# Shifted tokens as whole rows in their own tile, a quarter of the sine products on VectorE, and a new order of steps, in a twelve-layer local-attention stage

## The chip, the cores and the metric

The kernel runs on one core of one Trainium2 chip. A core has five engines with an instruction queue each, and every queue is worked off in order: TensorE (PE in the profile, with its weight loads as PEld), VectorE (DVE), ScalarE (ACT), GpSimd (POOL) and SyncE (SP). SP only starts transfers here; POOL starts some too. Sixteen DMA engines carry the transfers. Matrix products go to PSUM, which this kernel uses as eight banks of 512 numbers in each of 128 partitions; everything else lies in SBUF. The metric is the device time of one execution in microseconds (us). The kernel before took 4753.31 us (median of 3 runs, 4749.81 to 4759.05).

## The reference, cut to what matters

The input x is four sequences of 512 tokens of 128 numbers, in float32. The parts in their order: a mixture-of-experts feed-forward and a linear attention (the front), a stack of six local-attention layers, a full attention of sixteen heads, and the six-layer stack once more. The second and the last part are the same code, and they are where the change lies. One layer of it is

```python
def shift_tokens(t):
    a, s = jnp.split(t, 2, -1)
    s = jnp.pad(s, ((0, 0), (1, 0), (0, 0)))[:, :-1]
    return jnp.concatenate([a, s], -1)
...
q = l2norm(q) * qs
k = l2norm(k) * ksc
...
q = q * cos * scale + rotate_half(q) * sin * scale
k = k * cos * inv + rotate_half(k) * sin * inv
out = local_attention(q, k, v)
...
for i in range(DEPTH):
    x = attn_layer(shift_tokens(x), Wqkv[i], q_scale[i], k_scale[i], Wo[i]) + x
    x = ffn_layer(shift_tokens(x), ln_g[i], ln_b[i], W1[i], b1[i], W2[i], b2[i]) + x
```

Two things matter below. Each sublayer reads numbers 0 to 63 of a token and numbers 64 to 127 of the token before it, with zeros for the token before the first. And queries and keys get a rotary embedding: the projection times a cosine table, plus the projection of the partner number times a sine table.

## The kernel before, in words

**Data.** `x[b]` is a tile of 128 partitions by 4 by 128: token 128·t + p of sequence b lies in partition p, row t. So the token before lies one partition higher up, except for partition 0, which needs partition 127 of row t - 1.

**Work.** A layer is worked off for each sequence b in two halves `hf` of eight heads. Each half is a `Unit`, whose methods are generators of steps (a `yield` ends a step):

- `proj(c)`, c = 0 to 7: chunk c of the keys (c = 0 to 3, s = 0) or queries (c = 4 to 7, s = 1). Step 0 makes three matmuls (lines 279 to 281) into a PSUM bank; step 1 copies the bank to the tile `raw` (ACT, line 305); step 2 squares it (ACT, `sq`, line 308); step 3 multiplies the bank by the cosine table (DVE, line 313, into `rtk` or `rtq`); step 4 multiplies `raw` by the sine table (POOL, line 315).
- `swap(s)`: two transfers started by POOL (line 395) add `raw`, with even and odd partitions exchanged, onto `rtk` or `rtq`. It needs all four chunks of s.
- `norm`, `norm_q`: lengths of keys and queries (matmuls of lines 326 and 360 into bank `n2`, a transpose on DVE, logarithm and exponential on ACT, corrections on DVE, lines 342 to 347). `spread` multiplies the keys by their inverse lengths (line 386 on PE, line 389 on DVE).
- `score(k, h)`: masks and scores (lines 425 and 434) into the one bank pair `S`; `soft(k)`: softmax (DVE lines 444 and 446, POOL 449, ACT 451, DVE 454 and 456, POOL 458, DVE transpose 461).
- `vproj(i)`: values, already multiplied by the output weights (PE 407, ACT copy 413); `out(k)`: attention times values (PE 477); `add`: onto `x[b]` (DVE 484).

After both halves of a sequence a `Ffn` follows. Its step `stats` 0 has SP start two transfers that fetch the shifted half of the tokens (lines 606 and 607); step 1 takes means and variances (DVE, lines 612, 614, 615); step 2 the logarithm and exponential (ACT, line 618); step 3 normalizes (POOL, lines 624 to 633); steps 4 to 6 transpose (PE 637, ACT 640, DVE 642). Then come `gate`, `gelu`, `lin` (three steps each, the last one into bank `fout`, line 685) and `fadd` (DVE 692), which frees the bank of `fout`.

**Buffers.** All matmul results but `n2`, `S` and `av` share four PSUM banks `mm` that go round in the order of the program. A step that takes a bank waits until the readers of the fourth result before it are done. `S` has one buffer: the next `score` waits until `soft` step 0 has read the last.

**Order.** For this stage the order is written out by hand. Each step has a due time in the table `TIMES`, by name and half, to which the position of the half in the sequence of halves is added; `Events.at` raises it to the time of every step that it waits for, and all steps are emitted in the order of the resulting times. Since every engine works its queue in order, this sets what stands behind what. Steps of one sequence overlap with those of the next: while the feed-forward of sequence b begins, the second half of sequence b + 1's attention is under way. One period of this order, one sequence in one layer, is two halves; there are 48 periods.

Of the kernel before, what the change touches and what calls it, by code (L numbers as in the profile page):

```python
# [6 lines left out]
F32 = mybir.dt.float32  # L7
# [3 lines left out]
ALU = mybir.AluOpType  # L11
# [109 lines left out]
def setup_l1(g, c):  # L121

    nc, P = g.nc, g.const
# [15 lines left out]

    g.wp = g.ctx.enter_context(g.tc.tile_pool(name="l1w", bufs=1))  # L140
# [4 lines left out]
    def fill():  # L145
# [4 lines left out]
        nc.gpsimd.memset(g.ge2[64:128], 1.0)  # L150
        NEG = -1.0e25
# [132 lines left out]
class Unit:  # L284
# [8 lines left out]
    def proj(self, c):  # L293
        g = self.g
        nc = g.nc
        xT = g.xT[(self.l, self.b)]
        s, i = c // 4, c % 4
        ps = bank(g, "mm", [128, 512], "qkps")
# [5 lines left out]
        raw = self.raw[s][:, i, :]  # L304
        nc.scalar.copy(raw, ps)  # L305
# [6 lines left out]
        rot = g.rot[(self.l, s)]  # L312
        nc.vector.tensor_tensor(self.rt[s][:, i, :], ps, rot[:, 0, :], ALU.mult)  # L313
        yield
        nc.gpsimd.tensor_tensor(raw, raw, rot[:, 1, :], ALU.mult)  # L315
# [171 lines left out]
    def events(self, ev, u):  # L487
# [3 lines left out]
        def go(fn, *args, **wait):  # L491
            ev.steps(u, (fn.__name__, hf) + args, (key, fn.__name__) + args, fn(*args),
                     {int(n[1:]): [x if isinstance(x[0], tuple) else (key,) + x for x in xs] for n, xs in wait.items()})

        P = ev.before
        for c in range(8):
            go(self.proj, c, s0=[((l, b), "xT", 2), ((l, hf), "qk", c, 2)],
               s1=[("proj", c // 4 * 4, 1)] if c % 4 else [],
               s3=[((l,), "rot", c // 4, 1)] + ([("proj", c // 4 * 4, 3)] if c % 4 else []))
# [3 lines left out]
        for s in range(2):  # L503
            go(self.swap, s, s0=[("proj", c, t) for c in range(4 * s, 4 * s + 4) for t in (3, 4)])
# [17 lines left out]
class Events:  # L522
# [30 lines left out]
    ('proj', 0, 0): (0.505, 0.505, 0.505, 0.505, 0.505), ('proj', 1, 0): (0.375, 0.375, 0.375, 0.406, 0.406),  # L553
    ('proj', 0, 1): (0.789, 0.789, 0.789, 0.789, 0.789), ('proj', 1, 1): (0.582, 0.582, 0.582, 0.582, 0.582),
    ('proj', 0, 2): (0.722, 0.722, 0.722, 0.722, 0.722), ('proj', 1, 2): (0.466, 0.466, 0.466, 0.466, 0.466),
    ('proj', 0, 3): (0.728, 0.728, 0.728, 0.728, 0.728), ('proj', 1, 3): (0.339, 0.375, 0.375, 0.406, 0.406),
    ('proj', 0, 4): (0.925, 0.925, 0.925, 0.925, 1.025), ('proj', 1, 4): (0.795, 0.795, 0.795, 0.795, 0.795),
    ('proj', 0, 5): (1.063, 1.063, 1.063, 1.063, 1.353), ('proj', 1, 5): (0.901, 0.901, 0.901, 0.901, 0.901),
    ('proj', 0, 6): (0.961, 0.961, 0.961, 0.961, 0.961), ('proj', 1, 6): (0.668, 0.795, 0.795, 0.795, 0.795),
    ('proj', 0, 7): (1.072, 1.072, 1.072, 1.072, 1.072), ('proj', 1, 7): (0.932, 0.932, 0.932, 0.932, 1.330),  # L560
    ('norm', 0): (1.020, 1.020, 1.112, 1.337, 1.337, 1.443), ('norm', 1): (0.843, 0.843, 0.843, 0.971, 1.057, 1.197),
    ('norm_q', 0): (1.466, 1.492, 1.492, 1.701, 1.701), ('norm_q', 1): (1.079, 1.571, 1.571, 1.754, 1.754),
    ('swap', 0, 0): (0.789,), ('swap', 1, 0): (0.582,), ('swap', 0, 1): (1.353,), ('swap', 1, 1): (1.330,),
    ('spread', 0, 0): (1.443, 1.443), ('spread', 1, 0): (1.582, 1.586), ('spread', 0, 1): (1.443, 1.443),
    ('spread', 1, 1): (1.443, 1.443), ('spread', 0, 2): (1.443, 1.443), ('spread', 1, 2): (1.197, 1.197),
    ('spread', 0, 3): (1.660, 1.660), ('spread', 1, 3): (1.197, 1.197), ('score', 0, 0, 0): (1.838,),
    ('score', 1, 0, 0): (1.881,), ('score', 0, 0, 1): (1.838,), ('score', 1, 0, 1): (1.881,),
    ('soft', 0, 0): (1.838, 2.074, 2.074, 2.074, 2.376, 2.565),
    ('soft', 1, 0): (1.881, 1.881, 2.044, 2.119, 2.119, 2.230), ('score', 0, 1, 0): (2.034,),
    ('score', 1, 1, 0): (2.044,), ('score', 0, 1, 1): (2.034,), ('score', 1, 1, 1): (2.044,),  # L570
    ('soft', 0, 1): (2.034, 2.301, 2.415, 2.415, 2.415, 2.586),
    ('soft', 1, 1): (2.044, 2.044, 2.171, 2.171, 2.243, 2.243), ('vproj', 0, 0): (1.875, 1.875),
    ('vproj', 1, 0): (2.169, 2.169), ('vproj', 0, 1): (2.135, 2.135), ('vproj', 1, 1): (2.169, 2.169),
    ('vproj', 0, 2): (2.135, 2.135), ('vproj', 1, 2): (2.261, 2.261), ('vproj', 0, 3): (2.135, 2.339),
    ('vproj', 1, 3): (2.261, 2.261), ('vproj', 0, 4): (2.135, 2.339), ('vproj', 1, 4): (2.261, 2.261),
    ('vproj', 0, 5): (2.428, 2.428), ('vproj', 1, 5): (2.261, 2.261), ('vproj', 0, 6): (2.428, 2.428),
    ('vproj', 1, 6): (2.261, 2.261), ('vproj', 0, 7): (2.428, 2.428), ('vproj', 1, 7): (2.261, 2.261),
    ('out', 0, 0): (2.839,), ('out', 1, 0): (2.422,), ('out', 0, 1): (2.839,), ('out', 1, 1): (2.422,),
    ('out', 0, 2): (2.839,), ('out', 1, 2): (2.422,), ('out', 0, 3): (3.161,), ('out', 1, 3): (2.422,),
    ('add', 0): (3.161,), ('add', 1): (2.422,), ('stats',): (2.828, 2.828, 2.828, 2.828, 3.037, 3.037, 3.037),  # L580
    ('gate', 0): (3.443, 3.443), ('lin', 0): (3.894, 3.894, 4.830), ('gate', 1): (3.443, 3.443),
    ('lin', 1): (3.894, 3.894, 4.830), ('gate', 2): (3.894, 3.894), ('lin', 2): (4.055, 4.055, 4.830),
    ('gelu',): (3.894,), ('aside',): (1.053,), ('fadd',): (4.830,), ('xT',): (-0.063, -0.063, 0.230),
    ('fw',): (4.307, 4.347, 4.347, 4.347), ('rot', 0): (-5.173, -5.173), ('rot', 1): (0.853, 0.853),
    ('qk', 0, 0): (-0.273, -0.273, -0.273), ('qk', 1, 0): (-0.135, -0.135, -0.135),
    ('qk', 0, 1): (-0.266, -0.266, -0.266), ('qk', 1, 1): (-0.287, -0.287, -0.287), ('qk', 0, 2): (0.033, 0.033, 0.208),
    ('qk', 1, 2): (0.405, 0.405, 0.405), ('qk', 0, 3): (-2.849, -1.272, -1.272), ('qk', 1, 3): (-0.698, -0.698, -0.698),
    ('qk', 0, 4): (0.366, 0.366, 0.366), ('qk', 1, 4): (-0.246, -0.246, -0.246), ('qk', 0, 5): (-1.224, -0.937, -0.937),
    ('qk', 1, 5): (0.637, 0.637, 0.637), ('qk', 0, 6): (-0.738, -0.738, -0.738), ('qk', 1, 6): (0.271, 0.271, 0.271),
    ('qk', 0, 7): (-1.136, -0.928, -0.928), ('qk', 1, 7): (0.767, 0.767, 0.767), ('lvo', 0): (1.549,),  # L590
    ('lvo', 1): (1.889,), ('vo', 0, 0): (1.549, 1.549), ('vo', 1, 0): (1.889, 1.889), ('vo', 0, 1): (1.549, 1.549),
    ('vo', 1, 1): (1.889, 1.889),
# [3 lines left out]
class Ffn:  # L596
# [4 lines left out]
    def stats(self):  # L601
        g = self.g
        nc, xb = g.nc, g.x[self.b]
        xs = tile_of(g, "xs", [128, 4, 64], F32, "xs")
        nc.vector.memset(xs[0:1, 0, :], 0.0)
        nc.sync.dma_start(out=xs[1:128], in_=xb[0:127, :, 64:128])
        nc.sync.dma_start(out=xs[0:1, 1:4, :], in_=xb[127:128, 0:3, 64:128])
# [757 lines left out]
```

## Time and profile before

| | |
|---|---|
| runs | 4749.81, 4753.31, 4759.05 us |
| the profiled execution | 4747.36 us, span 4745.6 us, granted PE clock 0.903 |
| PE busy | 3911.9 us, 82% |
| DVE, ACT, POOL busy | 3077.8, 2666.3, 2687.7 us |
| the two six-layer stages | about 600 to 2390 and 2935 to 4746 us from the start |

The profile is that of one execution; times in it are counted from the start of its span. A group of instructions is a line of the kernel with its engine, the tiles it writes and reads, its count, its busy time and mean duration, and what ended the idle time before it. The chain that ended last is followed back from the end: at each step to the instruction or transfer that released it. The view of waits adds up idle time by who waited for whom. PEclk is the share of PE's full clock that was granted. Where successive instructions of an engine overlap a little, their spacing is smaller than their duration, and sums along a path go by the spacing.

In the stage of interest, 300 us of it (3303 to 3603) hold PE 250.5, DVE 184.9, ACT 172.6 and POOL 199.7 us of work.

### The profile page before, as it was taken

Reading aid. Unit: us, or ns where it says so; the run is one execution under the profiler, and the core shown is the slowest. Engines: PE = TensorE matmul, PEld = TensorE weight load, DVE = VectorE, ACT = ScalarE, POOL = GpSimd, SP = SyncE. Lnnn points to the kernel's source line nnn. Section 1 sums busy time; section 2 is a strip of 40 time slices with the busy share of each in tenths; the row PEclk is TensorE's granted clock in tenths of the full one; section 3 lists DMA queues with packets and bytes.
Section 4 is the critical chain, followed back from the end, with each engine's and each line's share of the span. In section 5 each row is a group of like instructions: output and inputs, shape, how many; then the busy total and the mean of one; then the engine's idle time right before and its main releaser. Section 6 shows DMA issues by size and latency. Waiting matters only on the chain.

```text
span 4745.6 us, 150287 instructions
## 1 busy us (share of the span) xinstructions
PE 3911.9 (82%) x66374; PEld 2632.2 (55%) x66436; DVE 3077.8 (65%) x5759; ACT 2666.3 (56%) x5242; POOL 2687.7 (57%) x2630
## 2 busy tenths in 40 slices
PE   8989878788787888888769998878888788787876
PEld 5666556555565555656523333556556555555654
DVE  6968856566565666656668885656656556665665
ACT  4434455556565555655536676555656555565653
POOL 4625576667666666666500002666676666766664
PEclk9989989898898989989879998989989898898988
DMA  2000043333333333333332222334233342323331
GB/s 57 18 9 19 28 99 69 80 63 72 78 63 81 72 72 72 68 77 73 68 80 63 71 68 54 70 68 87 58 85 68 68 85 60 83 61 72 83 68 42
DMA packets 163854, 312.47 MB, mean 66 GB/s; under 512 B 41304, under 2 KB 125664, under 8 KB 138176
## 3 DMA queue, kind: packets, MB, share of 16 engines
q0 software_dynamic: 31008, 202.40, 21.8%
q1 hardware_dynamic: 132192, 100.44, 7.5%
q8 instruction: 521, 8.54, 0.7%
q14 instruction: 133, 1.09, 0.1%
HBM read 77.49 MB, written 17.69 MB: 20 GB/s over the span
## 4 chain that ended last, share of the span: by engine, by line
PE 41%; DMA 19%; DVE 19%; ACT 7%; POOL 7%; issue 6%; SPq 0%; POOLq 0%; ACTq 0%; DVEq 0%
DMA xs<-x 18%; PE vps L407 11%; PE av L477 5%; PE S L434 3%; DVE h L944 3%; DVE E L446 3%; DVE mx L444 3%; PE av L1193 3%; POOL raw L315 2%; PE S L1156 2%; PE n L360 2%; POOL E L458 2%; PE ST L1185 2%; ACT raw L305 2%; ACT sq L308 1%
## 5 line engine op out<-in xcount | busy, mean ns | idle before, releaser
L315 POOL TENSOR_TENSOR raw<-raw,rot 128x512 f32<-128x512 f32 x768 | 1036.0, 1433 | 300.4 <-ACT raw L305 300.4
L407 PE MATMUL vps<-vo,xF 128*32 128x256 f32 x12288 | 787.4, 408 | 57.1 <-DVE ge L679 43.1
L413 ACT COPY vx<-vps 128x512 f32<-128x512 f32 x768 | 445.4, 588 | 413.6 <-PE vps L407 404.8
L407 PEld LDWEIGHTS vps<-vo,xF 128*32 128x32 f32 x12288 | 427.2, 119 | 351.6 <-issue 86.7
L305 ACT COPY raw<-qkps 128x512 f32<-128x512 f32 x768 | 455.7, 593 | 236.7 <-PE qkps L281 231.0
L458 POOL TENSOR_TENSOR E<-E,smr 128x1024 f32<-128x1024 f32 x192 | 391.0, 2070 | 151.4 <-ACT vx L413 90.3
L308 ACT ACTIVATE sq<-qkps 128x512 f32<-128x512 f32 x768 | 475.9, 620 | 0.0
L389 DVE TENSOR_TENSOR rtk<-rtk,R 128x512 f32<-128x512 f32 x384 | 248.4, 678 | 319.9 <-PE R L386 319.9
L449 POOL TENSOR_TENSOR E<-E,rq 128x1024 f32<-128x1024 f32 x192 | 367.9, 1916 | 134.7 <-DVE E L446 129.4
L313 DVE TENSOR_TENSOR rtk<-qkps,rot 128x512 f32<-128x512 f32 x384 | 258.1, 683 | 212.7 <-ACT sq L308 210.2
L477 PE MATMUL av<-vx,pt 128*32 128x128 f32 x11904 | 367.7, 274 | 18.0 <-DVE pt L461 11.8
L1157 DVE TENSOR_REDUCE nm<-S 128x1 f32<-128x512 f32 x512 | 337.4, 686 | 63.9 <-PE S L1156 59.3
L279 PE MATMUL qkps<-xT,wqk 128*128 128x512 f32 x768 | 337.2, 439 | 43.6 <-DVE rtk L313 22.7
L477 PEld LDWEIGHTS av<-vx,pt 128*32 128x32 f32 x11904 | 326.8, 110 | 75.8 <-issue 39.0
L1186 ACT ACTIVATE E<-ST 128x512 f32<-128x512 f32 x512 | 280.4, 595 | 127.3 <-PE ST L1185 103.3
L434 PE MATMUL S<-rtk,rtq 64*32 64x64 f32 (+1 forms) x24576 | 316.0, 243 | 33.8 <-issue 32.0
L313 DVE TENSOR_TENSOR rtq<-qkps,rot 128x512 f32<-128x512 f32 x384 | 255.0, 682 | 133.4 <-ACT sq L308 133.4
L434 PEld LDWEIGHTS S<-rtk,rtq 64*32 64x32 f32 x24576 | 302.2, 114 | 58.8 <-issue 48.0
L618 ACT ACTIVATE y<-bmv,eps 128x4 f32<-128x4 f32 x48 | 14.3, 297 | 564.7 <-DVE bmv L615 564.7
L946 POOL TENSOR_TENSOR h<-r,h 128x512 fp32r<-128x512 f32 x128 | 182.0, 1422 | 252.5 <-DVE h L944 238.5
L280 PE MATMUL qkps<-xT,wqk 128*128 128x512 f32 x768 | 307.9, 401 | 4.3 <-POOL xT L274 2.4
L614 DVE BATCH_NORM_STATS2 bst<-xs 128x6 f32<-128x64 f32 x192 | 35.8, 186 | 424.6 <-DMA xs<-x 424.6
(259 smaller groups left out, 8755.9 us busy)
## 6 DMA issues: line engine op xcount, KB each, us to landing
rtk<-raw POOLq DMA_DIRECT2D x192, 512.0 KB, 7.0
rtq<-raw POOLq DMA_DIRECT2D x192, 512.0 KB, 6.2
pd<-pc SPq DMA_DIRECT2D x36, 384.0 KB
rot<-in_c_rot SPq DMA_DIRECT2D x24, 512.0 KB
wqkr<-in_L_ffn_Wqk SPq DMA_DIRECT2D x192, 64.0 KB
k<-pd SPq DMA_DIRECT2D x32, 288.0 KB
r<-in_L_ffn_W SPq DMA_DIRECT2D x32, 256.0 KB
wvraw<-in_L_ffn_WvT SPq DMA_DIRECT2D x24, 256.0 KB
```

Source lines behind the costliest of these rows:

```text
L279: nc.tensor.matmul(out, lhsT=wh, rhs=xh, start=True, stop=False)
L305: nc.scalar.copy(raw, ps)
L308: nc.scalar.activation(sq, ps, AF.Square)
L313: nc.vector.tensor_tensor(self.rt[s][:, i, :], ps, rot[:, 0, :], ALU.mult)
L315: nc.gpsimd.tensor_tensor(raw, raw, rot[:, 1, :], ALU.mult)
L407: nc.tensor.matmul(ps[p * 32:(p + 1) * 32, ww, :], lhsT=xF[:, t0:t0 + 32], rhs=g.vo[(self.l, self.hf, p // 2)][:, p % 2, :], start=True, s ...
L413: nc.scalar.copy(self.v[th][:, 2 * t:2 * t + 2, :], ps)
L434: nc.tensor.matmul(self.S[k][p * 32:(p + 1) * 32, ab, w * 64 + 64 - n:w * 64 + 64], lhsT=self.rt[1][rows, p, t0:t0 + 32], rhs=self.rt[0][r ...
L449: nc.gpsimd.tensor_tensor(E4, E4, self.rq[:, :, 8 * k:8 * k + 8].unsqueeze(3).to_broadcast([128, 2, 8, 64]), ALU.mult)
L458: nc.gpsimd.tensor_tensor(E, E, r.unsqueeze(2).to_broadcast([128, 16, 64]), ALU.mult)
L477: g.nc.tensor.matmul(self.av[ww * 32:(ww + 1) * 32, k, :], lhsT=self.pt[w // 8][:, ab, w % 8, role, :], rhs=self.v[src // 8][:, src % 8, a ...
L1157: nc.vector.tensor_reduce(self.nm[:, h, qt:qt + 1], S, AX.X, ALU.max, negate=True)
```

## The change

It does three things. The diff, with the table of due times cut:

```diff
+    g.xs = P.tile([128, 4, 128], F32, name="xs")
...
+        nc.gpsimd.memset(g.xs[0:1, 0, :], 0.0)
...
     def proj(self, c):
...
-        nc.scalar.copy(raw, ps)
+        if i == 3:
+            nc.vector.tensor_tensor(raw, ps, g.rot[(self.l, s)][:, 1, :], ALU.mult)
+        else:
+            nc.scalar.copy(raw, ps)
...
-        nc.gpsimd.tensor_tensor(raw, raw, rot[:, 1, :], ALU.mult)
+        if i < 3:
+            nc.gpsimd.tensor_tensor(raw, raw, rot[:, 1, :], ALU.mult)
...
-               s1=[("proj", c // 4 * 4, 1)] if c % 4 else [],
+               s1=([("proj", c // 4 * 4, 1)] if c % 4 else []) + ([((l,), "rot", c // 4, 1)] if c % 4 == 3 else []),
...
-            go(self.swap, s, s0=[("proj", c, t) for c in range(4 * s, 4 * s + 4) for t in (3, 4)])
+            go(self.swap, s, s0=[("proj", c, t) for c in range(4 * s, 4 * s + 4) for t in (1, 3, 4)])
...
 TIMES = {
...
-    ('proj', 0, 7): (1.072, 1.072, 1.072, 1.072, 1.072), ('proj', 1, 7): (0.932, 0.932, 0.932, 0.932, 1.330),
-    ('norm', 0): (1.020, 1.020, 1.112, 1.337, 1.337, 1.443), ('norm', 1): (0.843, 0.843, 0.843, 0.971, 1.057, 1.197),
+    ('proj', 0, 7): (0.877, 0.764, -0.313, -1.740, -2.999), ('proj', 1, 7): (1.084, -4.129, -7.230, 0.644, -5.232),
+    ('norm', 0): (0.762, -1.476, -2.205, 1.133, -0.091, 1.172),
+    ('norm', 1): (0.878, -4.677, -1.901, 1.124, 1.149, 1.233), ('norm_q', 0): (1.132, -6.229, 0.890, 1.433, -3.078),
...
 }
...
     def stats(self):
         g = self.g
         nc, xb = g.nc, g.x[self.b]
-        xs = tile_of(g, "xs", [128, 4, 64], F32, "xs")
-        nc.vector.memset(xs[0:1, 0, :], 0.0)
-        nc.sync.dma_start(out=xs[1:128], in_=xb[0:127, :, 64:128])
-        nc.sync.dma_start(out=xs[0:1, 1:4, :], in_=xb[127:128, 0:3, 64:128])
+        nc.sync.dma_start(out=g.xs[1:128], in_=xb[0:127])
+        nc.sync.dma_start(out=g.xs[0:1, 1:4, :], in_=xb[127:128, 0:3, :])
+        xs = g.xs[:, :, 64:128]
         yield
```

The fetch of the shifted tokens was 127 partitions of 4 pieces of 256 bytes and is now 127 partitions of one row of 2048 bytes; half of what arrives isn't read. The second, small fetch was 3 pieces of 256 bytes and stands in the built program as 16 pieces of 96 bytes. The tile is set to zero in row 0 once, and no longer for each sequence.

Of every four chunks of keys or queries the fourth (i = 3) no longer has a copy on ACT and a sine product on POOL; DVE multiplies it by the sine table straight from PSUM.

Every due time is new. Due times below that of an awaited step only mean "as soon as that step has been emitted". The built program has the same instructions on PE, 192 fewer on ACT and on POOL, 192 more sine products on DVE, and another order. For the stretch of a period between `add` of the second half of sequence b (call it hf 1; hf 0' and hf 1' are those of sequence b + 1) and the length matmuls `norm_q` of hf 1', the queues hold:

- PE before: spread 0, 1, 2 and norm_q of hf 0'; proj 2, 1 of hf 1'; spread 3; proj 6, 4; `fout` of b - 1; score 0 of hf 0'; norm of hf 1'; vproj 0 of hf 0'; proj 5, 7; the transposes of the sequence b + 2; score 1 of hf 0'; the transposes of `stats` 4; norm_q of hf 1'.
- PE after: spread 3 of hf 0'; proj 1 of hf 1'; spread 1; proj 4, 6; the transposes of b + 2; spread 0; norm of hf 1'; vproj 0 and score 0 of hf 0'; `fout` of b - 1; proj 7, 5; score 1; the transposes of `stats` 4; norm_q of hf 1'. (norm_q of hf 0', proj 2 and one spread stand before `out` now.)
- DVE before: three spreads, cosines 2 and 1, spread 3, cosines 6 and 4, then `stats` 1; after it `fadd`, soft 0 step 0 of hf 0', the transpose of norm, cosines 5 and 7, soft 1 step 0, `stats` 6, norm step 4.
- DVE after: spread 3 and 1, cosine 1, cosines 4 and 6, spread 0, the transpose of norm, then `stats` 1; after it soft 0 step 0 of hf 0', `fadd`, the sine of chunk 7, cosines 7 and 5, soft 1 step 0, `stats` 6, norm step 4.
- POOL: the swap of hf 0's queries comes before `add` in both; between it and the swap of hf 1's keys stand the sine products 0, 3, 2, 1 before, and 0, 2, 1 after (in both lists "hf 0's" and "hf 1's" are hf 0' and hf 1').
- SP: the fetches stand right after the `add` that they wait for. In two periods of four, weight loads (`wqkr`) stand directly before the fetch in both programs, though not the same ones.

## The prediction

> **What bounds the kernel now.** I read the page first, then the waits, then one period by engine, then the transfers. The page, the waits, and the instructions around one fetch of the shifted tokens (SP, DVE and PE of the timeline):
>
> ```profile
> PE 3911.9 (82%) x66374; PEld 2632.2 (55%) x66436; DVE 3077.8 (65%) x5759; ACT 2666.3 (56%) x5242; POOL 2687.7 (57%) x2630
> ...
> PE 41%; DMA 19%; DVE 19%; ACT 7%; POOL 7%; issue 6%; SPq 0%; POOLq 0%; ACTq 0%; DVEq 0%
> ```
>
> ```profile
> DVE bst L614 <- DMA xs<-x: 424.6, 48, 9.8
> ...
> PE xTps L264 <- DVE x L692: 230.6, 42, 7.7
> ...
> PE n L360 <- DVE zt L346: 147.5, 48, 5.5
> ...
> PE S L425 <- DVE E L446: 98.2, 49, 10.4
> ```
>
> ```profile
> 3303.29 0.74 SPq L606 DMA_DIRECT2D xs<-x  x1
> 3304.07 12.30 SPq L607 DMA_DIRECT2D xs<-x  x1
> ```
>
> ```profile
> 3320.63 0.23 DVE L614 BATCH_NORM_STATS2 bst<-xs 128x6 f32<-128x64 f32 x1 [8.87 <-DMA xs<-x]
> ```
>
> ```profile
> 3322.71 0.66 PE L264 MATMUL xTps<-ident,x 128*128 128x128 f32 x4 [1.72 <-DVE x L692]
> 3325.10 0.63 PE L425 MATMUL S<-mask,msel 64*32 64x512 bf16 x8 [1.74 <-DVE E L446]
> ...
> 3331.51 1.94 PE L360 MATMUL n<-sq,sums 128*32 128x128 f32 x32 [2.91 <-DVE zt L346]
> 3333.22 5.60 PE L407 MATMUL vps<-vo,xF 128*32 128x256 f32 x64
> ```
>
> PE is the fullest engine, and outside one place it hardly waits. The place comes once in each of the 48 periods: SP starts the fetch, and 17.3 us later DVE gets it. DVE, ACT and POOL have reached their steps of `stats` by then and stand. PE goes on until it needs DVE, and then waits three times, which are the three PE rows of the waits: 230.6 + 147.5 + 98.2 = 476 us, 9.9 us per period. The period shown has 11.2 us of PE idle in all, 2.0 of it away from the fetch. The stretch after the stall is slow as well:
>
> ```profile
> 3303.00:3313.00 10.00, 9.69 (x218) 7.79 (x217) 6.43 (x17) 4.71 (x11) 6.99 (x8) 1.00 0.57 113
> 3313.00:3321.00 8.00, 5.37 (x38) 2.59 (x29) 0.34 (x2) 0.00 (x0) 0.62 (x1) 0.79 0.58 127
> 3321.00:3332.00 11.00, 4.64 (x156) 3.61 (x160) 9.68 (x22) 6.78 (x15) 8.89 (x14) 0.62 0.06 19
> 3332.00:3340.00 8.00, 8.00 (x104) 4.94 (x96) 2.00 (x4) 3.16 (x6) 5.88 (x5) 0.67 0.57 114
> ```
>
> (Columns: length, busy time of PE, PEld, DVE, ACT, POOL, granted clock, DMA share, GB/s.) In the last two rows the clock is 0.62 and 0.67, and 64 value matmuls take 5.60 us where 112 take 6.25 in warm stretches.
>
> So a period is a sum of three: the fetch L (in 46 of 48 periods 17.0 to 18.8 us, two values in turn, about 17.3 and 18.5; mean 17.8), then 10.97 us to norm_q (3320.54 to 3331.51), then 46.6 us in which PE is nearly full, to the next fetch at 3378.12. That makes 74.8, and 23 periods from 670.37 average 74.6.
>
> **The fetch itself.** What does L consist of? The last fetch has no swap beside it and takes 10.3 us:
>
> ```profile
> DMA packets 516, 0.15 MB, mean 15 GB/s; under 512 B 515, under 2 KB 515, under 8 KB 515
> ## 3 DMA queue, kind: packets, MB, share of 16 engines
> q1 hardware_dynamic: 515, 0.13, 6.6%
> ```
>
> 6.6% of sixteen engines is 1.06 engines: the 508 pieces go through one engine, one after the other. By the single packet records the first moves 1.4 us after the issue, all take 8.1 us (15.9 ns each; 14.3 when nothing else runs), and 0.6 us pass to the use. In a steady period there come on top: the end of the query swap on that engine (1.6 to 2.5 us), the key swap, 8 packets of 629 ns = 5.0 us, and an instruction fetch (0.9 us). 10.2 + 7.1 to 8.4 gives the two values above.
>
> **The change, part by part.**
>
> *Whole rows.* 127 rows of 2048 bytes, again 127 partitions; I estimate one engine again. No row of before shows 2 KB pieces from SBUF to SBUF. Nearest are the reads of `xo` near the end: median 84 ns for 2 KB. Below: an 8 KB load packet takes 307 ns, so 77 for a quarter. Above: in the busiest microsecond of `xo` 66 packets hold 72.1% of 16 engines, 175 ns each. I take 80, since short packets start 4 ns before the last ends: 127 x 80 = 10.2 us against 8.1, so +2.1 us (77 gives +1.7, 175 would give +14). A lower end for everything: if the price were per piece, 127 x 15.9 = 2.0 us, -6.1. Bytes double, pieces fall to a quarter; the rows 18 ns (256 B), 27 (512 B), 84 (2 KB), 109 (2.7 KB) grow with bytes, so I stay with +2.1.
>
> The Trainium skill, "DMA: Bandwidth & Descriptors", asks for pieces of at least 512 bytes for line rate (Specifications), which speaks for the change. The same page, section "Why a DMA increments its semaphore by 16 and not by 1", says that 127 partitions put a transfer on a single engine, which the 6.6% above shows, and this speaks against it. Taken alone, the first with sixteen engines at the page's 27 GiB/s each would make about 0.6 us of the rows, L near 5 and 450 us less; the second at that rate makes 9.0 us, an estimate, which is 1.2 us per period, 58 us in all, under my sum.
>
> *What meets the fetch.* After the change I place the query swap's issue 5.4 us before the fetch (its POOL work ends earlier relative to `add`) instead of 3.0 to 4.2; it lasts 8.1 us on that engine, so its end costs about 0.9 us and not 1.6 to 2.5. The key swap needs only three sine products before it, and is issued 2.4 us after the fetch instead of 6: 5.0 us fully inside, as before. L = 1.4 + 0.9 + 10.2 + 5.0 + 0.5 (half an instruction fetch) + 0.6 = 18.6, so +0.8 on 17.8.
>
> *The order before the landing.* By the queues and the rows' spacings (proj 0.70 on PE; raw and sq 0.97 on ACT; cosine 0.65, spread 0.63 on DVE; fout 2.94; score 1.85), DVE reaches `stats` 6.1 us after the fetch (before 8.5), ACT 6.5, POOL 7, and PE runs dry at 11.3 (before at 17.7). The transposes of x no longer stand behind `fadd`: the 230.6 us wait goes. Late next is score 1, which needs S, read by soft 0 behind the fetch: one wait of L + 3.9 - 11.3 = 11.2 us. A fetch of 6 to 7 us would suit this order; each us above it is paid.
>
> *From landing to norm_q.* Means 1.45, maximum and difference 2.45, fadd 0.6, sine of chunk 7 0.65, square 0.6 (line 313 starts when the square ends, 210.2 and 133.4 us of its waits; I take the two readers of a bank to go one after the other), cosines 7 and 5 with their wait 1.6, maximum and difference 2.4, `xnT` 0.6, corrections 0.95: 11.3 against 10.97, +0.4. If the square need not wait, -0.2; if fadd and the sine did not stand there, 1.2 less.
>
> *norm_q to the next fetch.* PE's list, priced as above, gives 45.2 and 0.6 of waits: 45.8, where before has 46.0 with its share of weight work evened out: -0.2. This includes 2.1 us of PE work (norm_q of hf 0', proj 2, a spread) that stood in the stall before. The bound of a gain is the 2.0 us that PE idles there; of a loss, I take 2.0 too: in my walk the last softmax transpose ends 0.2 us before `out` needs it, so nothing covers a delay.
>
> *The sine products.* 192 x 1.25 us leave POOL (240 us), 192 x 0.48 ACT (92), 192 x 0.68 come to DVE (131). POOL stands idle for the fetch anyway, so its gain is worth nothing there; without the stall it would be worth up to 5 us a period on the swaps. Of the four DVE products a period, one is on the path (counted); three lie beside `out` and the projections, where DVE's list is 3.6 us against PE's 3.7. *SP*: loads moved past the fetch are issued in 0.37 us each; they wait for POOL work that is done; if not, each us late is one us in that period. The row of zeros saves 48 x 0.11 us on DVE, beside the wait.
>
> Sum: +0.8 + 0.4 - 0.2 = +1.0 us x 48 = +48 on the profiled execution's 4747.4, which is 6 us under the median: **4800 us**.
>
> **Rivals.**
> *A, faster: the fetch is over before the key swap reaches its engine.* In before, that engine starts the key swap about 2.8 us after the other fifteen, some 170 pieces later. If pieces and not bytes are what stand in line, all 127 rows go first: L = 18.6 - 5.0 = 13.6, 48 x (-4.2 + 0.2) = -192: 4560. It decides below L = 17.6, where the sum is zero. For it: the 170 pieces. Against: once both are moving, they alternate one by one.
> *B, slower still: the engines that now stand earlier start late elsewhere*, +2.0 us a period in the third stretch: 4895. For it: no cover there. Against: PE fills that stretch in both orders.
> *C: nothing happens.* L stays at 17.8 and the order pays back the sine: 4753.
> *D: the rows spread over many engines.* By the records the 128 rows of `xo` pass in 1.6 us, which makes L = 1.4 + 0.9 + 1.6 + 0.5 + 0.6 = 5.0; the stall goes, 74.6 - 9.6 = 65 us a period, 48 x -9.6 = -461: 4290. Against: 127 partitions, as before.
>
> **How the numbers follow.** Forecast 0.42 (its own range 4750 to 4860), A 0.32, B 0.15, C 0.06, D 0.05. Three runs differ by 0.2%, about what can be told from no change. Faster: A, D and 0.04 of the forecast, 0.41; same: C and 0.02 of it, 0.08; slower 0.51. The range leaves out D, half of B's far end and A's low end: 4555 to 4910.
>
> **What would show it.** Right: DVE's wait for the fetch grows from 424.6 to about 600 us; PE's wait for `fadd` is gone and that of the score masks for DVE grows from 98 to about 500; DMA records of 2048 bytes, 1 engine's worth; POOL near 2450, DVE near 3200. L near 13 with the swap behind it is A; 2 KB pieces on many engines are D; a fetch as priced with PE waiting elsewhere is B. My walk of the queues is by hand; an error of 1 us a period is 48 us.

## The result, and the profile after

The changed kernel takes 4962.34 us (median of 4 runs, 4954.91 to 4966.66) where the kernel before, run beside it, takes 4756.18 (4749.81 to 4763.84). The ratio is 1.0431, with a 95% interval of 1.041 to 1.0452: 206 us slower, 162 us above the forecast of 4800 and outside its range. The profiled execution took 4962.51 us, with a span of 4960.7 and a granted clock of 0.889 (before 0.903).

The page of the changed kernel, its engines and its chain of work (share by engine, then by line):

```profile
PE 3912.4 (79%) x66374; PEld 2642.0 (53%) x66436; DVE 3217.3 (65%) x5903; ACT 2550.9 (51%) x5050; POOL 2442.3 (49%) x2439
...
PE 34%; DVE 25%; DMA 19%; ACT 14%; issue 6%; POOL 2%; SPq 0%; DVEq 0%; ACTq 0%; POOLq 0%
DMA xs<-x 17%; PE vps L414 9%; ACT sq L314 5%; DVE h L952 3%; ACT raw L311 3%; DVE mx L451 3%; PE av L1201 2%; PE S L1164 2%; DVE raw L309 2%; PE n L367 2%; DVE E L453 2%; POOL E L465 2%; DVE pt L468 2%; PE ST L1193 2%; PE av L484 2%
```

PE's busy time is what it was, 3912 us, so the loss is idle time of PE: 834 us of the span before, 1048 after. In the chain PE fell from 41% to 34%, while DVE rose from 19% to 25% and ACT from 7% to 14%; ACT's square (L314) holds 5% of it, where its share before was 1%, and DVE's new product (L309) 2%. The waits of the changed kernel (who waited, for whom; total us, times, longest):

```profile
DVE bst L622 <- DMA xs<-x: 617.5, 48, 13.7
ACT sq L314 <- DVE raw L309: 489.8, 192, 5.1
PE S L432 <- DVE E L453: 470.2, 49, 14.4
...
PE n L367 <- DVE zt L353: 192.5, 48, 8.2
...
ACT n L346 <- DVE qt L371: 134.5, 48, 3.1
PE vps L414 <- ACT vx L420: 107.2, 47, 2.7
```

Three of these were foreseen: DVE's wait for the fetch, PE's for the softmax at the score masks, and the transposes' wait for `fadd` gone (the group `xTps` no longer stands behind it). Two were not: ACT's square waits for DVE's product 192 times, and PE waits once in each period for a value copy by ACT. The instructions around one fetch of the changed kernel (timeline; SP, DVE and PE):

```profile
3433.78 0.65 SPq L613 DMA_DIRECT2D xs<-x  x1
3434.48 8.20 SPq L614 DMA_DIRECT2D xs<-x  x1
...
3452.23 0.23 DVE L622 BATCH_NORM_STATS2 bst<-xs 128x6 f32<-128x64 f32 x1 [13.46 <-DMA xs<-x]
...
3456.10 0.63 PE L432 MATMUL S<-mask,msel 64*32 64x512 bf16 x8 [7.50 <-DVE E L453]
...
3463.40 1.92 PE L367 MATMUL n<-sq,sums 128*32 128x128 f32 x32 [3.81 <-DVE zt L353]
```

The same period by windows (length, busy time of PE, PEld, DVE, ACT, POOL, granted clock, DMA share, GB/s): to the stall, the stall, to norm_q, and the value matmuls after it. DVE, ACT and POOL stand still in the second row, and the clock after the stall is 0.69 and 0.79.

```profile
3433.80:3444.80 11.00, 8.28 (x191) 5.85 (x190) 4.53 (x11) 5.04 (x10) 5.88 (x7) 0.92 0.52 107
3444.80:3452.30 7.50, 3.80 (x20) 3.17 (x19) 0.07 (x1) 0.00 (x0) 0.00 (x0) 0.89 0.28 87
3452.30:3463.40 11.10, 3.49 (x140) 2.73 (x140) 9.81 (x22) 4.16 (x10) 8.62 (x13) 0.69 0.14 29
3463.40:3471.40 8.00, 7.85 (x112) 5.62 (x112) 2.88 (x5) 3.75 (x7) 4.43 (x3) 0.79 0.50 100
```

The transfers of the last fetch, which has no swap beside it, in the changed kernel:

```profile
DMA packets 160, 0.26 MB, mean 20 GB/s; under 512 B 33, under 2 KB 33, under 8 KB 160
## 3 DMA queue, kind: packets, MB, share of 16 engines
q1 hardware_dynamic: 160, 0.26, 5.8%
```

5.8% of sixteen is 0.93 engines: the rows go through one engine, as the pieces did. By the packet records the 127 rows take 11.4 us, 90 ns each.

Split as in the prediction, and averaged over the 46 periods inside the two stages (us; L runs from the issue of the fetch to DVE's first instruction on what it brings):

| | fetch L | landing to norm_q | norm_q to next fetch | period |
|---|---|---|---|---|
| before | 17.82 | 11.07 | 45.47 | 74.36 |
| forecast | 18.6 | +0.4 | 45.8 (-0.2) | +1.0 |
| after | 18.21 | 11.38 | 48.96 | 78.55 |

The third stretch holds +3.5 of the +4.2 us a period; 48 x 4.2 = 201 us is nearly the whole loss.

### The profile page after: what moved, and what is told of

It reads as the page before. It is cut to its first block, busy times and chain, and to the rows that moved or that the text cites. A ratio compares the mean times of both kernels' runs of the same rounds, so it can differ in the third digit from the quotient of the medians.

```text
span 4960.7 us, 150057 instructions
## 1 busy us (share of the span) xinstructions
PE 3912.4 (79%) x66374; PEld 2642.0 (53%) x66436; DVE 3217.3 (65%) x5903; ACT 2550.9 (51%) x5050; POOL 2442.3 (49%) x2439
## 4 chain that ended last, share of the span: by engine, by line
PE 34%; DVE 25%; DMA 19%; ACT 14%; issue 6%; POOL 2%; SPq 0%; DVEq 0%; ACTq 0%; POOLq 0%
DMA xs<-x 17%; PE vps L414 9%; ACT sq L314 5%; DVE h L952 3%; ACT raw L311 3%; DVE mx L451 3%; PE av L1201 2%; PE S L1164 2%; DVE raw L309 2%; PE n L367 2%; DVE E L453 2%; POOL E L465 2%; DVE pt L468 2%; PE ST L1193 2%; PE av L484 2%
## 5 line engine op out<-in xcount | busy, mean ns | idle before, releaser
L322 POOL TENSOR_TENSOR raw<-raw,rot 128x512 f32<-128x512 f32 x576 | 736.7, 1289 | 365.7 <-ACT raw L311 334.2
L314 ACT ACTIVATE sq<-qkps 128x512 f32<-128x512 f32 x768 | 470.4, 612 | 489.8 <-DVE raw L309 489.8
L420 ACT COPY vx<-vps 128x512 f32<-128x512 f32 x768 | 426.5, 592 | 389.4 <-PE vps L414 382.2
L432 PE MATMUL S<-mask,msel 64*32 64x512 bf16 x1536 | 88.8, 439 | 470.5 <-DVE E L453 470.2
L622 DVE BATCH_NORM_STATS2 bst<-xs 128x6 f32<-128x64 f32 x192 | 35.8, 186 | 617.5 <-DMA xs<-x 617.5
L456 POOL TENSOR_TENSOR E<-E,rq 128x1024 f32<-128x1024 f32 x192 | 414.1, 2269 | 14.2 <-DVE E L453 10.9
L311 ACT COPY raw<-qkps 128x512 f32<-128x512 f32 x576 | 339.9, 590 | 79.0 <-PE qkps L284 76.4
L282 PE MATMUL qkps<-xT,wqk 128*128 128x512 f32 x768 | 337.7, 440 | 37.9 <-ACT xT L274 14.7
L319 DVE TENSOR_TENSOR rtq<-qkps,rot 128x512 f32<-128x512 f32 x384 | 265.1, 690 | 121.9 <-ACT sq L314 114.6
L367 PE MATMUL n<-sq,sums 128*32 128x128 f32 x3072 | 159.4, 346 | 194.5 <-DVE zt L353 192.5
```

What stands on the lines that cost most here:

```text
L282: nc.tensor.matmul(out, lhsT=wh, rhs=xh, start=True, stop=False)
L314: nc.scalar.activation(sq, ps, AF.Square)
L420: nc.scalar.copy(self.v[th][:, 2 * t:2 * t + 2, :], ps)
L456: nc.gpsimd.tensor_tensor(E4, E4, self.rq[:, :, 8 * k:8 * k + 8].unsqueeze(3).to_broadcast([128, 2, 8, 64]), ALU.mult)
```

## The experiments

**The three parts, each alone and two together.** They come from the two kernels by undoing or adding whole parts. Theory "order" was that the new table makes the third stretch longer by itself, theory "sine" that DVE's product ahead of ACT's square does.

`order`: before, with the new table of times.

```diff
 TIMES = {
-    ('proj', 0, 0): (0.505, 0.505, 0.505, 0.505, 0.505), ...
+    ('proj', 0, 0): (0.413, -1.552, -9.694, -5.544, -3.573), ...
```

> The kernel before with the changed kernel's table of times and nothing else: fetch of 256-byte pieces, all sine products on POOL. Of the changed kernel's +4.2 us per period, +3.5 lie between norm_q and the next fetch, which neither the rows nor the fetch can reach. Theory order (the new order alone makes that stretch longer, by placing ACT's copies behind steps that wait for DVE, and by moving PE work there): that stretch 48.5 to 49.5 us against 45.5, the period 77.5 to 79, 4900 to 4960 us. Theory sine (the stretch is longer since ACT's square stands behind DVE's new product): the stretch stays at 45 to 46.5 and the time at 4720 to 4800.

`sine`: before, with the part of the diff that concerns i == 3 and its waits.

```diff
-        nc.scalar.copy(raw, ps)
+        if i == 3:
+            nc.vector.tensor_tensor(raw, ps, g.rot[(self.l, s)][:, 1, :], ALU.mult)
+        else:
+            nc.scalar.copy(raw, ps)
```

> The kernel before with the sine products of chunks 3 and 7 made by DVE from PSUM, and nothing else. Theory sine: the wait of ACT's square for the DVE product appears (of the order of 490 us, as in the changed kernel), the stretch from norm_q to the next fetch grows by 2 to 3.5 us, 4850 to 4920 us. Theory order: ACT may wait, but nobody waits for ACT; the stretch stays within 0.5 us of 45.5 and the time between 4720 and 4780 us.

`rows`: before, with whole rows into a tile of their own.

```diff
-        nc.sync.dma_start(out=xs[1:128], in_=xb[0:127, :, 64:128])
+        nc.sync.dma_start(out=g.xs[1:128], in_=xb[0:127])
```

> The kernel before with the shifted tokens fetched as whole rows into a tile of their own, and nothing else. By the prediction's sum the fetch takes 127 rows x 80 ns + the two swaps' share: L 18.2 to 19.5 us against 17.8 (the lone fetch at the end 13.0 against 10.3), the other two stretches unchanged within 0.3 us: 4770 to 4840 us. Theory 'rows are longer on the engine, but start sooner because SP issues 130 elements and not 511': L 17.4 to 17.9, 4735 to 4755 us.

The pairs are the changed kernel with one part taken back: `rows_order` without the sine, `rows_sine` without the new table, `sine_order` without the rows.

> The changed kernel with all sine products on POOL again (rows and order stay). Theory order: still slow, the stretch from norm_q to the next fetch 48.5 to 49.5 us, 4920 to 4980 us. Theory sine: that stretch back to 45.5 to 46.5, 4780 to 4850 us.

> The changed kernel with the table of times of the kernel before (rows and sine stay). Theory order: the stretch from norm_q to the next fetch 45 to 46 us; 4750 to 4820 us. Theory sine: that stretch 47.5 to 49.5, 4860 to 4960 us.

> The changed kernel with the fetch of the kernel before (256-byte pieces); sine and order stay. If the rows cost what the prediction priced, L falls from 18.2 to 16.5 to 17.8 us and the time from 4962 to 4880 to 4945 us. If the fetch's length is set by the swaps, L and the time stay: 18.0 to 18.5 us, 4950 to 4970 us.

Measured (time of the run, ratio to the kernel before run beside it with its interval, and the stretches):

| run | us | ratio | L | to norm_q | to next fetch | period |
|---|---|---|---|---|---|---|
| order | 4686.18 | 0.9877 [0.9862, 0.9892] | 14.92 | 10.46 | 47.28 | 72.66 |
| sine | 4808.77 | 1.0127 [1.0109, 1.0145] | 18.11 | 11.37 | 46.03 | 75.51 |
| rows | 4863.39 | 1.024 [1.0224, 1.0255] | 20.26 | 11.06 | 45.33 | 76.65 |
| rows_order | 4846.25 | 1.021 [1.0195, 1.0226] | 18.16 | 10.58 | 47.18 | 75.92 |
| rows_sine | 4925.97 | 1.0382 [1.0367, 1.0398] | 20.48 | 11.38 | 46.21 | 78.07 |
| sine_order | 4807.47 | 1.0135 [1.0118, 1.0152] | 14.98 | 11.38 | 49.01 | 75.36 |

Neither theory had it right. The order alone is a gain: it takes 2.9 us off the fetch, which neither expected, and gives 1.8 back in the third stretch. The rows touch L alone: +2.4 in the old order, +3.2 in the new. The sine is the part that changes with its surroundings: +1.15 us a period in the old order, +2.70 in the new one, of which 1.73 in the third stretch. So the +3.5 of that stretch is 1.8 from the order and 1.7 from the sine in that order. My expectations of `rows` (L up to 19.5) and `sine_order` (L at least 16.5) were both too low a price for the rows.

Why the order shortens the fetch can be read from the transfers. Before, the query swap is issued 4.2 us ahead of the fetch (median of the 46 periods) and its last 8 KB packet ends 4.1 us after the fetch's issue; in `order` it is issued 7.6 us ahead and ends 0.5 us before the issue. What is left on the fetch is the key swap.

ACT's wait is not a price by itself. In `sine`, in the old order, it is as long as in the changed kernel:

```profile
ACT sq L311 <- DVE raw L306: 512.7, 190, 4.1
```

and the third stretch grows by 0.56 us only. There PE's matmuls wait for ACT's value copies 0.18 us a period in that stretch; in `order` they wait 2.0 us and in the changed kernel 2.3.

**Where the sine costs.** `late_order`: run `order`, with DVE's product moved to step 4, behind ACT's square and DVE's cosine.

```diff
-        nc.scalar.copy(raw, ps)
+        if i < 3:
+            nc.scalar.copy(raw, ps)
...
-        nc.gpsimd.tensor_tensor(raw, raw, rot[:, 1, :], ALU.mult)
+        if i == 3:
+            nc.vector.tensor_tensor(raw, ps, rot[:, 1, :], ALU.mult)
+        else:
+            nc.gpsimd.tensor_tensor(raw, raw, rot[:, 1, :], ALU.mult)
```

> Run order (new table of times, old fetch, 72.66 us a period) plus the DVE sine products, but at step 4, behind ACT's square and DVE's cosine, where POOL made them; step 1 of these chunks does nothing. Run sine_order, with the product at step 1 ahead of the square, has 75.36 us a period and 4807 us. Theory square (the product costs because ACT's square of the same bank stands behind it): the 490 us wait of ACT's square for DVE is gone, 72.7 to 73.8 us a period, 4690 to 4740 us. Theory DVE (0.68 us on DVE cost wherever they stand, since DVE brings `add` and norm's step 4 later): 74.8 to 75.8 us, 4780 to 4830 us.

Measured: 4638.66 us, ratio 0.9762 [0.9747, 0.9776], 71.81 us a period. The same 192 products on the same engine cost 2.70 us a period at step 1 and gain 0.85 at step 4. Theory DVE falls, and theory square is exceeded: what remains without the wait is ACT's relief from the copies, as I read it; no run tells ACT's relief from POOL's.

`a_late`: the same move in the changed kernel itself.

> The changed kernel with one move: DVE's sine products at step 4 of their chunk, behind ACT's square and the cosine, in place of step 1. Theory square (the wait for the square is the missing term): the period falls from 78.55 us to about that of rows_order (75.92) less the 0.85 that late_order gained on order: 75.1 us, 4790 to 4815 us, which is the forecast's time. Theory 'DVE's late arrival is the term': 77.5 to 78.5 us, 4915 to 4960 us.

Measured: 4794.55 us, ratio 1.0082 [1.0065, 1.0099], L 18.18, 10.54 and 46.44, 75.15 us a period. This is the forecast's time, within 6 us, but in part by chance: against the forecast its fetch is 0.4 us shorter, the second stretch 0.8 shorter and the third 0.6 longer. The step that the product stands in is worth 168 us. What it does can be read in the changed kernel's timeline, at one chunk of keys and at one `add`:

```profile
3483.16 1.23 DVE L453 TENSOR_TENSOR E<-S,mx 128x1024 f32<-128x1024 f32 x1
3484.30 0.31 DVE L371 STREAM_TRANSPOSE qt<-n 128x128 f32<-128x128 f32 x1
3484.53 0.65 DVE L309 TENSOR_TENSOR raw<-qkps,rot 128x512 f32<-128x512 f32 x1
3485.22 0.60 ACT L314 ACTIVATE sq<-qkps 128x512 f32<-128x512 f32 x1 [5.08 <-DVE raw L309]
3485.85 0.69 DVE L319 TENSOR_TENSOR rtk<-qkps,rot 128x512 f32<-128x512 f32 x1 [0.66 <-ACT sq L314]
```

```profile
3431.20 0.59 ACT L314 ACTIVATE sq<-qkps 128x512 f32<-128x512 f32 x1
3431.83 0.69 DVE L319 TENSOR_TENSOR rtk<-qkps,rot 128x512 f32<-128x512 f32 x1 [0.58 <-ACT sq L314]
3432.44 0.68 DVE L396 TENSOR_TENSOR rtk<-rtk,R 128x512 f32<-128x512 f32 x1
3433.03 0.68 DVE L491 TENSOR_TENSOR x<-x,av 128x512 f32<-128x512 f32 x1
3433.78 0.65 SPq L613 DMA_DIRECT2D xs<-x  x1
```

The product, the square and the cosine read one PSUM bank, and go one after the other: DVE, ACT, DVE. At step 1 the product stands in DVE's queue behind softmax work, ACT stands for it 5.08 us with all its copies behind it, and DVE then waits for ACT in turn. In the second fence `add` (L491) has no wait before it: the attention values were ready, DVE was not. Over the periods `add` starts 0.67 us (median) after PE's last `av` matmul in the changed kernel and 0.06 us after it in `a_late`; the fetch waits for `add`, so the period is longer by that. The answering rows of `a_late`, timeline and waits:

```profile
3330.06 0.69 DVE L491 TENSOR_TENSOR x<-x,av 128x512 f32<-128x512 f32 x1 [0.73 <-PE av L484]
3330.81 0.65 SPq L613 DMA_DIRECT2D xs<-x  x1
```

```profile
DVE rtk L317 <- ACT sq L312: 218.6, 188, 7.1
ACT sq L312 <- PE qkps L284: 33.8, 40, 1.6
```

The square no longer waits for DVE; what it waits for is PE, 34 us in all. Of the 2.52 us that `a_late` takes off the third stretch, PE's waits are 1.11 (3.18 to 2.07) and the later `add` 0.6. Another 0.34 is in norm_q of hf 0', whose matmuls take 1.35 us in the changed kernel and 1.01 in `a_late`, at a granted clock of 0.96 in both: the last square that they read ends 0.28 us after the first of them has started, in `a_late` 0.9 us before it. norm_q of hf 1', after the stall, gives 0.18 (1.91 us against 1.73, at a clock of 0.51 and 0.61). About 0.3 us are not accounted for.

The Trainium skill, "PSUM — Partial Sum Buffer", section "PSUM bank collisions raise a hardware error", says why they go in turn: no two engines may access one bank in the same partitions at the same time, two readers included, and the back end orders them. The 192 waits agree; no run here lets two engines read at once.

**Where the order's 1.8 us come from.** PE's work in the third stretch (its length less PE's waits) grows from 42.90 us (before) to 44.77 (`order`), near the 2.1 us that the prediction had. But PE's waits stay: 2.57 before, 2.51 in `order`, 2.05 in `late_order`, where the prediction left 0.6. The largest in the new order is the value matmuls' wait for ACT, once in a period: 2.0 us of the 2.51 in `order`. `lo_pt`: run `late_order` with one due time moved, so that DVE makes norm_q's transpose before a softmax transpose and not after it.

```diff
-    ('soft', 1, 0): (-3.251, -8.273, 1.894, 0.171, -1.509, 2.103),
+    ('soft', 1, 0): (-3.251, -8.273, 1.894, 0.171, -1.509, 2.1325),
```

> Run late_order with one step moved on DVE: in each period one softmax transpose (pt) stands behind the transpose of norm_q (qt) and no longer ahead of it. Theory 'ACT's norm step holds the bank copies': in the timeline of order qt ends 1.3 us sooner, ACT's square into the bank n2, the value copies behind it and PE's wait for them (1.5 us a period in late_order) come sooner by that: 0.8 to 1.4 us a period less, 4570 to 4605 us. Rival 'another bank reader is late next' (the copies meet PE's pace anyway): within 0.3 us a period, 4625 to 4650 us.

Measured: 4578.41 us, ratio 0.9633 [0.9619, 0.9647]; third stretch 45.20, PE's waits in it 0.74, 70.63 us a period (-1.18). PE's wait for the value copies over the whole run, in `late_order` and in `lo_pt`:

```profile
PE vps L411 <- ACT vx L417: 70.7, 47, 1.8
```

```profile
PE vps L411 <- ACT vx L417: 7.0, 21, 0.7
```

The same place in `late_order` and then in `lo_pt` (timeline):

```profile
3444.75 1.25 DVE L465 STREAM_TRANSPOSE pt<-E 128x1024 f32<-128x1024 f32 x1 [0.17 <-POOL E L462]
3445.92 0.27 DVE L368 STREAM_TRANSPOSE qt<-n 128x128 f32<-128x128 f32 x1
3446.29 0.20 ACT L343 ACTIVATE n<-ky 128x32 f32<-128x32 f32 x1 [2.86 <-DVE qt L368]
3446.43 3.22 ACT L417 COPY vx<-vps 128x512 f32<-128x512 f32 x6
3447.06 1.93 PE L411 MATMUL vps<-vo,xF 128*32 128x256 f32 x32 [1.60 <-ACT vx L417]
```

```profile
3480.49 0.30 DVE L368 STREAM_TRANSPOSE qt<-n 128x128 f32<-128x128 f32 x1
3480.74 1.25 DVE L465 STREAM_TRANSPOSE pt<-E 128x1024 f32<-128x1024 f32 x1
3480.89 0.20 ACT L343 ACTIVATE n<-ky 128x32 f32<-128x32 f32 x1 [1.47 <-DVE qt L368]
3481.02 3.22 ACT L417 COPY vx<-vps 128x512 f32<-128x512 f32 x6
```

ACT's square writes into the bank `n2`, which `qt` reads; six value copies stand behind it, and PE's matmuls need the banks they free. In `late_order` a 1.2 us transpose ahead of a 0.3 us one cost PE 1.3 us in every period.

**One engine, or sixteen.** `a_split` and `split_b` are the kernel after and the one before with the fetch in two transfers.

```diff
-        nc.sync.dma_start(out=xs[1:128], in_=xb[0:127, :, 64:128])
+        nc.sync.dma_start(out=xs[1:113], in_=xb[0:112, :, 64:128])
+        nc.sync.dma_start(out=xs[113:128], in_=xb[112:127, :, 64:128])
```

> The changed kernel with the 127 rows fetched by two DMAs, one of 112 partitions and one of 15, in place of one of 127; nothing else. Theory one engine (127 partitions cannot be shared out, so one DMA engine carries all rows): 112 partitions go to 16 engines and 15 to 15, about 8 rows each; beside the swaps' packets of 0.63 us, one for one, that is 8 x 0.71 = 5.7 us and a start of 1.4: L 5 to 8.5 us against 18.2. DVE then reaches its wait at about 6 us: the period falls by 9 to 11 us, 4430 to 4540 us. Theory 'the swaps set it' (rows wait for the swaps' packets on whichever engine): L 13 to 18, 4720 to 4960 us.

> The kernel before with its fetch of 127 partitions in two DMAs, of 112 and 15 partitions; nothing else. Theory one engine: the 508 pieces of 256 bytes go over 16 engines, 28 to 32 each. By themselves 32 x 16 ns = 0.5 us; if each also waits for one packet of a swap (0.63 us), the fetch ends when the swaps do, 1.4 + 0.9 + 5.0 us and up to 3 more: L 6 to 11 us, 4250 to 4440 us. Theory 'the issue on SP sets it' (12.3 us of SP for 511 elements): L stays above 14 us and the time above 4600 us.

`ro_split` is `a_split` with all sines on POOL; `o_split` and `r_split` are the split with the new order alone and with the rows alone.

> Rows and new order, all sine products on POOL, the rows fetched in two DMAs of 112 and 15 partitions: run a_split without the DVE sine. Theory 'the sine is a cost in any case': its 2.6 us a period, measured with the long fetch, come off a_split's 67.99: 65 to 66 us, 4300 to 4360 us. Theory 'POOL's relief counts once no engine stands for the fetch' (the prediction put it at up to 5 us a period): 68 to 72 us, 4445 to 4640 us.

> New order alone, with the 256-byte pieces fetched in two DMAs of 112 and 15 partitions: run order with the split, or ro_split with pieces in place of rows. Theory 'pieces wait for swap packets one for one': 28 to 32 pieces on each engine, so L 6.5 to 9.5 us where rows have 5 to 5.5; DVE arrives 5.6 us after the issue, so 1 to 4 us a period more than ro_split: 66 to 69 us, 4340 to 4480 us. Theory 'hidden': within 20 us of ro_split.

> The kernel before with whole rows and the fetch in two DMAs of 112 and 15 partitions, old order, no DVE sine: split_b (L 8.92, 66.29 us a period, 4366 us) with rows in place of pieces. L 5 to 7 us. In the old order DVE arrives about 8.5 us after the issue, so theory 'the walk's arrival time is the floor' expects almost nothing for the shorter fetch: 65.8 to 66.3 us, 4340 to 4370 us. Theory 'L counts in full': 63 to 64 us, 4200 to 4260 us.

| run | us | ratio | L | to norm_q | to next fetch | period |
|---|---|---|---|---|---|---|
| a_split | 4443.66 | 0.9366 [0.9351, 0.9381] | 5.23 | 13.58 | 49.18 | 67.99 |
| split_b | 4366.25 | 0.9205 [0.9185, 0.9226] | 8.92 | 12.32 | 45.05 | 66.29 |
| ro_split | 4375.80 | 0.9209 [0.919, 0.9227] | 5.79 | 13.22 | 47.17 | 66.18 |
| o_split | 4381.80 | 0.9224 [0.9205, 0.9242] | 5.85 | 13.18 | 47.12 | 66.15 |
| r_split | 4369.36 | 0.9199 [0.9184, 0.9215] | 8.94 | 12.22 | 45.16 | 66.32 |

The last fetch of `split_b` (transfers, in a window of 3.2 us from its issue):

```profile
DMA packets 546, 0.15 MB, mean 46 GB/s; under 512 B 545, under 2 KB 545, under 8 KB 545
...
q1 hardware_dynamic: 545, 0.13, 20.8%
```

The pieces are through 3.1 us after the issue, where the one transfer needed 9.5; in steady periods, too, the last piece or row of the two transfers ends 2.5 us after the issue (median) in `a_split`, `ro_split` and `o_split`, and 4.7 in `split_b`. So the one engine made the fetch long, and once it is cut pieces or rows make no difference: 6 us between `ro_split` and `o_split`, 3 between `r_split` and `split_b`. One theory of `o_split` had the pieces lose 1 to 4 us a period beside the swaps; in that run they are through at 2.5 us, and the key swap's first packet starts at 4.2. In these runs L is DVE's own time of arrival, 5.0 to 8.5 us after the issue (medians); its waits for the fetch are 5.4 us in all in `a_split` and 5.8 in `split_b`. The sine still costs 1.8 us a period there (`a_split` less `ro_split`), less than the 2.6 expected, so `ro_split` ended 16 us above its range; relief of POOL did not turn it into a gain.

The Trainium skill, "DMA: Bandwidth & Descriptors", section "Why a DMA increments its semaphore by 16 and not by 1", states that a transfer uses the largest number of engines up to 16 that divides the slowest dimension on both of its sides, and has 127 partitions on one engine as an example; 16 engines for 112 partitions and 15 for 15 are worked out from that rule. The shares of this case, 5.8 and 6.6% for the one transfer against 20.8% for the two, fit it; no view here numbers the engines.

**Put together.** `o_split_late_pt`: new order, pieces in two transfers, late sine, and the moved transpose. `b_split_late`: the kernel before with the two transfers and the late sine.

> New order, 256-byte pieces in two DMAs of 112 and 15 partitions, late DVE sine, and the moved transpose; nothing else. o_split has 66.15 us a period and 4382 us. If the late sine (-0.85) and the moved transpose (-0.8 to -1.4) count in full: 63.9 to 64.5 us, 4275 to 4310 us. If the late sine relieves POOL, which without the stall feeds the swaps: up to 2 us more, 4180 to 4275 us. If DVE is the next bound (DVE busy 3200 of 4300 us): 66 us, 4360 to 4390 us.

> The kernel before with its fetch in two DMAs and the late DVE sine; old order. split_b has 66.29 us a period and 4366 us, and DVE arrives at its wait 8.5 us after the issue, in which the sines of two chunks now would stand. Theory 'the late sine frees ACT and POOL': 65 to 66 us, 4310 to 4350 us. Theory 'DVE is the floor in this order' (no engine waits for POOL or ACT there): 66.3 to 67.5 us, 4366 to 4430 us.

`o_split_late_pt` takes 4279.37 us, ratio 0.9001 [0.8988, 0.9015], 64.44 us a period, and is faster than both kernels. Against `o_split` it gains 1.71 us a period, where the late sine (0.85) and the moved transpose (1.18) had made 2.03 with the long fetch. `b_split_late` takes 4390.45, ratio 0.9238 [0.9222, 0.9255], 66.80 us a period, where `split_b` has 0.9205 and 66.29: no gain, and by the period a loss (the intervals of the two ratios just touch). A new wait of its POOL is the likely cause; the first line is `split_b`, the second `b_split_late`:

```profile
POOL rtq L395 <- POOL raw L315: 28.2, 95, 0.3
```

```profile
POOL rtq L399 <- DVE raw L317: 321.1, 47, 9.5
```

POOL starts the query swap, and now waits for DVE's late product. `o_split_late_pt` has no such wait. No run takes the wait away by itself, so its share of the loss is not shown; of the two orders tried, the late sine gained in the new one alone.

## Why the prediction was wrong

- **The step that failed** is *norm_q to the next fetch*: "45.2 and 0.6 of waits: 45.8 ... -0.2". It was 48.96. The PE work in it was right for the order (`order` has 44.77 us). The 0.6 of waits was not: `order` has 2.51 and the changed kernel 3.18. The walk by hand followed PE's list and took ACT's and DVE's as keeping up; it missed that `qt` behind `pt` holds ACT, and six copies with it (`lo_pt`: 1.2 us a period), and that DVE's product ahead of the square holds ACT (`a_late`: 2.5 us in this stretch). With both out of the way, in `lo_pt`, the stretch is 45.20 us with 0.74 of waits, close to the walk's 45.8 and 0.6. The base was off as well: 46.0 for before came from the one period shown, and 46 periods average 45.47.
- **The sine products** were costed at "one is on the path (counted); three lie beside `out` and the projections, where DVE's list is 3.6 us against PE's 3.7". The sum of DVE's work was right and the conclusion wrong: here the two queues wait for each other, so that the fuller one covered nothing. The rule that two readers of a bank go one after the other was in the prediction, for chunk 7 after the landing, and was not carried to the other three chunks.
- **The fetch** came out within 0.4 us (18.6 forecast, 18.21 measured), by two errors. The rows were put at +2.1; the lone fetch shows 13.04 against 10.25, +2.8, and in the period +2.4 to +3.2, since a row took 90 ns and not 80 (the 77 given as a lower end came from the shortest 8 KB packet of before; their median is 619 ns). The swaps' and the instruction fetch's share was put 1.3 lower; it fell by 2.9 (`order`: 14.92, which is the lone 10.25 and 4.7, less than the 5.0 of the key swap alone). The query swap's end, 0.9 us in the sum, is not on that path any more: the prediction placed its issue 5.4 us before the fetch, and in the changed kernel it is issued 8.2 us before (median) and has ended 1.0 us before the fetch starts.
- **The weighed rule**, about 27 GiB/s an engine by the Trainium skill, "DMA: Bandwidth & Descriptors", Specifications, gave an estimate of 9.0 us for the rows; 11.4 were measured, so the row of the trace (10.2) was the nearer.
- **Landing to norm_q**: 11.3 forecast, 11.38 measured. The sine of chunk 7 ahead of its square costs 0.8 us there: with the product behind the square and the cosine the stretch is 10.54 (`a_late`), with it on POOL 10.58 (`rows_order`).
- **What would show it**: the forecast's list held (DVE's wait 617.5 for about 600, PE's wait at the masks 470 for about 500, `fadd`'s gone, POOL 2442, DVE 3217), and so did its sign for another case, "a fetch as priced with PE waiting elsewhere is B". B is what happened, at +3.5 us a period where it was priced at +2.0, which ended at 4895. Its "against", that PE fills that stretch in both orders, was the failed step again. Its chance of 0.15 was too small for a walk whose own error was said to be 48 us for each us.
- **Rivals A and D.** A falls: in the new order the key swap adds 4.7 us to the fetch of pieces and 5.1 to that of rows. D was priced at L 5.0 and 4290 us; it was not what the change does, but what the split makes of it: L 5.2 and 4444 us (`a_split`), or 5.8 and 4376 with the sines on POOL (`ro_split`).

## What to carry to other kernels

Before a product is moved to another engine, list who else reads its PSUM bank and in which order, and look up what stands ahead of it in the new engine's queue: here the step in which the same product stood was worth 168 us. A long wait of an engine is not the measure of that: ACT's 513 us in `sine` went with a loss of 1.15 us a period, and its 490 in the changed kernel with 2.63 (against `rows_order`), where PE waits longer for the value copies. An order that is laid out for the fullest engine must be walked for the others' queues too, since one short instruction behind a long one can be paid by whatever is queued behind its reader. And before a transfer's pieces are made larger, see over how many DMA engines it goes: cutting 127 partitions into 112 and 15 was worth 8%, the larger pieces nothing beside it and a loss of 2.4% without it.

## What the runs showed that was not expected

- The new table of times, which looks like the risk, was a gain by itself (61 us), and the whole rows, which look like the gain, cost 116 us alone and about 145 us beside the other parts (206 us of loss in the changed kernel, 61 in `sine_order`, each against the kernel before that ran beside it).
- The three parts don't add up: alone they come to +2.29, +1.15 and -1.70 us a period, together to +4.19. Most of the difference is the sine in the new order (2.70 in place of 1.15), the rest the rows in it (3.26 in place of 2.29).
- On one engine between two SBUF tiles, a 2048-byte row takes 90 ns where a 256-byte piece takes 15.9: eight times the bytes for 5.7 times the time (23 GB/s against 16).
- When the stall is gone the granted clock rises, from 0.903 to 0.95 in `split_b` and 0.946 in `o_split_late_pt`.
